# Four layers on one core: where v, the experts' mixing and the first images of layer 3 stand in PE's order

## The chip, the cores and the metric

The kernel runs on one core of a Trainium2 chip. Its engines work side by side and wait for each other through semaphores: PE (TensorE, matrix products), DVE (VectorE), ACT (ScalarE), POOL (GpSimd), and SP (SyncE), which here only issues DMAs. The metric is the time on the device in microseconds, the median of the runs; lower is better.

## The reference

Eight images of 512 channels and 32x32 positions go through four layers, all in f32. Cut to what matters here:

```python
# layer 0: attention with 8 heads, three tanh steps, projection
h = group_norm(x); q, k, v = split(qkv_w @ h + qkv_b)
h = softmax(q k^T * hd**-0.5) v
for _ in range(3): h = h + 0.1 * tanh(h @ inl_w.T + inl_b)
x = x + proj_w @ h + proj_b
# layer 1: one attention over all positions, and x added
x = softmax(q1(x)^T k1(x)) v1(x) + x
# layer 2: up by 2 in both directions (12 taps), leaky relu, down by 2
x = down(leaky_relu(up(x + bias), 0.2) * sqrt(2))
# layer 3: every image has its own weights, mixed from 8 experts
rw = sigmoid(mean(x, positions) @ router_w.T + router_b)     # 8 x 8
W = einsum('be,eoihw->boihw', rw, experts)                   # three convolutions
x = relu(bn3(conv1x1(relu(bn2(conv3x3(relu(bn1(conv1x1(x)))))))) + x)
```

## The kernel before

The program is one straight list for one core. The images are taken in turn through layers 0, 1 and 2. Images 0 to 6 are spilled to DRAM after layer 2; once the last one is through, layer 3 runs over all eight. (A second copy, L53, would run only where an exponential went out of bounds.)

Large products use a scheme of seven half-size products (P1, C11, U2, U3, C22, C21, C12). `product` (L524) does both halves u of each one; `in_turn` (L580) does all seven for u=0, then for u=1, so that its 14 parts can be handed out one by one. It opens one PSUM bank for each of the sums A, X and Y, from `ps_mm`, and yields after each part. U2 and U3 run on X, and U2 is read by DVE before U3 is added to it.

PSUM has three pools of two: `ps_sc` (pairs of banks, 128x1024), `ps_tp` and `ps_mm` (single banks, 128x512). SBUF's large tiles, of 128x4096 words, come from a pool of seven.

Inside `tc.manual_schedule` the order on the named engines is that of the program text. Outside it a planner orders each engine's work by its own costs; layer 0's tanh steps, its projection and layer 1 are such a part.

**Layer 2** (class `Layer2`, L1188) works on quarter tiles of the PE array, 32 or 64 rows by 32 or 64 columns, several of them side by side:

- `wide` (L1196) interpolates along one direction and stores to DRAM (`across`); `turn` (L1219) reads it back with the other direction on the partitions.
- `up` (L1226) interpolates the other direction into two `ps_sc` pairs; ACT multiplies by 0.2 and DVE takes the maximum (L1242, L1243), giving `fine`.
- `down` (L1245) filters and halves `fine` into two `ps_tp` banks; ACT and DVE copy them to `sent` (L1260), and SP stores `sent` in four DMAs to `back`. After four rows `turn_back` (L1267) reads `back` again.
- `narrow` (L1274) filters and halves the other direction into two `ps_tp` banks, which DVE copies (L1290). `channels` (L1292) transposes (`zT`) and sums for the router.

`fine_passes` (L1308) runs eight rows: `up` of row n, a fill, `down` of row n-1, a fill. A fill is one part of other work.

**Images 0 to 6.** `between` (L1324) runs layer 2 of image b and q, k, v of image b+1 in one order. q's parts stand by `wide`. k's 14 parts fill the fine passes, which have 18 fills. Then w_proj is loaded, and v's 14 parts stand around the `narrow` and `channels` passes.

**The last image.** `last_across` (L1375) does `wide` and has the router (L239) compute the gates of images 0 to 6. `last_rows` (L1399) runs the fine passes; their fills are pieces of `blend_early` (L294): 34 products of the gates with 512 columns of the experts' weights (mix, L300), copied by ACT and DVE in turn (L304) and stored by POOL's DMA (L305). `load_experts` reads the experts, 1792 KB at a time, into weight tiles. `last_columns` (L1413) does the narrow passes.

**Layer 3.** `load_weights` (L1479) reads an image's mixed weights, `transform_weights` (L1493) prepares them for the 3x3 convolution by sums of columns. Per image: `c1` (L1522, two halves), `spread` (L1531, four DVE sums of 128x544), four products `c2` (L1541), eight `c3` (L1550). An image's c1 stands in the image before it. The last image's own weights come from `blend_last` (L310), which reads the experts again, two tiles ahead, from products that stand in layer 3's first images.

Of the kernel before, what the change touches and what calls it, by code (L numbers as in the profile page):

```python
# [17 lines left out]
P = 128  # L18
# [39 lines left out]
def tile_sequence(ctx: ExitStack, tc: tile.TileContext, a: dict, out: bass.AP, shifted: bool):  # L58
# [156 lines left out]
    def late_loads():  # L215
# [10 lines left out]
        "early": const.tile([P, EARLY, NR], F32, name="blend_early"),  # L226
        "last": const.tile([P, 2, NR], F32, name="blend_last"),
    }
    nc.gpsimd.memset(blend["last"], 0.0)
    mixed = {  # L230
# [8 lines left out]
    class Router:  # L239
# [28 lines left out]
        def gates(self):  # L268
            at = rw[:, self.images, :]
            nc.scalar.activation(at, at, AF.Sigmoid)  # L270
# [10 lines left out]
    held_experts = []  # L281

    def load_experts():
        i = len(held_experts)
        n = min(len(PARTS) * HALF, WE - i * len(PARTS) * HALF)
        if n <= 0:
            return
        t = wpool.tile([P, len(PARTS), 2, QR], F32, tag="w", name=f"experts_{i}", bufs=3)
        t = t.rearrange("p a b c -> p (a b c)")
        at = i * len(PARTS) * HALF  # L290
        nc.sync.dma_start(t[:, 0:n], a["experts"][:, at : at + n])
        held_experts.append(t)

    def blend_early():  # L294
        rows = EARLY * NR
        op = blend["early"].rearrange("p b g -> p (b g)")
        for i in range(PIECES):
            n, at = divmod(i, len(PARTS))
            ps = bank(name=f"mix_{i}")
            nc.tensor.matmul(  # L300
                ps[0:rows, :], op, held_experts[n][:, ts(at, HALF)], start=True, stop=True
            )
            t = tmp(f"mix_{i}")
            (nc.scalar.copy if i % 2 else nc.vector.tensor_copy)(t[0:rows, :], ps[0:rows, :])  # L304
            nc.gpsimd.dma_start(mixed["early"][:, ts(i, HALF)], t[0:rows, :])  # L305
            if at == len(PARTS) - 1:
                load_experts()
            yield

    def blend_last():  # L310
        per = -(-PIECES // 4)
        op = blend["last"].rearrange("p b g -> p (b g)")
        tiles = {}

        def load(t):
            tiles[t] = big_tile(f"last_experts_{t}", [P, 4, 2 * HALF])
            for c in range(4):
                n = min(2, per - 2 * t, PIECES - per * c - 2 * t)
                if n > 0:
                    at = (per * c + 2 * t) * HALF  # L320
                    nc.sync.dma_start(
                        tiles[t][:, c, 0 : n * HALF], a["experts"][:, at : at + n * HALF]
                    )

        def counts(t):
            return [max(0, min(2, per - 2 * t, PIECES - per * c - 2 * t)) for c in range(4)]

        n_tiles = -(-per // 2)
        for t in range(2):
            load(t)  # L330
        yield
        for t in range(n_tiles):
            counted = counts(t)
            dst = tmp(f"mix_last_{t}", S)
            for i in range(2):
                if not counted[0] > i:
                    continue
                ps = bank(ps_tp, f"mix_last_{t}_{i}")
                last = 0
                for c in range(4):  # L340
                    if counted[c] > i:
                        nc.tensor.matmul(
                            ps[W * c : W * c + W, :], op, tiles[t][:, c, ts(i, HALF)],
                            start=True, stop=True,
                        )
                        last = W * c + W
                nc.scalar.copy(dst[0:last, ts(i, HALF)], ps[0:last, :])
                if i == counted[0] - 1:
                    for c in range(4):
                        n = counted[c] * HALF  # L350
                        at = (per * c + 2 * t) * HALF
                        if n:
                            nc.sync.dma_start(
                                mixed["last"][:, at : at + n], dst[W * c : W * c + NR, 0:n]
                            )
                    if t + 2 < n_tiles:
                        load(t + 2)
                yield
# [221 lines left out]
    def in_turn(name, wt, src, sums_of, made, rows=False, late=False):  # L580

        terms = {
# [8 lines left out]
        for u in range(2):  # L591
            banks = {}
            for what in plain if late and u == 0 else alternate:
# [6 lines left out]
                if what in opens:  # L600
                    banks[opens[what]] = bank(name=f"{name}_{opens[what]}{u}")
# [198 lines left out]
    def layer0(b, q, k, v, w):  # L800
# [193 lines left out]
        next(operators, None)  # L994
        all_of(inner)
        for it in (1, 2):
# [3 lines left out]
            for i, _ in enumerate(parts):  # L1000
                for _ in range(2 if i < 4 else 0):
                    next(operators, None)
        all_of(operators)
        if b + 1 < B:
            w["q"] = weight("q", b + 1)
        else:
            load_experts()
        t = quarter_sums(f"hf_{b}_3", hf)
        all_of(product(f"proj_{b}", w["proj"], hf, t, residual(f"proj_{b}", x)))
        if b + 1 < B:  # L1010
            w["k"] = weight("k", b + 1)
        else:
            load_experts()
        return x

    def layer1(b, x, w, x_next):
# [81 lines left out]
        else:  # L1098
            load_experts()
# [88 lines left out]
    class Layer2:  # L1188
# [85 lines left out]
        def narrow(self, e, i):  # L1274

            banks = [bank(ps_tp, f"narrow_{self.b}_{e}_{i}_{r}") for r in range(2)]
# [12 lines left out]
            for r in range(2):  # L1289
                nc.vector.tensor_copy(t[:, ts(r, HALF)], banks[r])  # L1290
# [17 lines left out]
        def fine_passes(self, fill=lambda: None):  # L1308
            order = [(e, i) for e in range(2) for i in range(4)]
            for n in range(len(order) + 1):  # L1310
                if n < len(order):
                    self.up(*order[n])
                fill()
                if n:
                    e, i = order[n - 1]
                    self.down(e, i)
                    if i == 3:
                        self.turn_back(e)
                fill()
# [4 lines left out]
    def between(b, eT, v, inv, y, x, mv, w):  # L1324
# [3 lines left out]
        with tc.manual_schedule(engines=hand):  # L1328
# [30 lines left out]
            two.fine_passes(lambda: next(parts, None))  # L1359
            all_of(parts)  # L1360
            w["proj"] = weight("proj", b + 1)
            v, parts = values(b + 1, x, t, w)
            steps = [(two.narrow, e, i) for e in (0, 1) for i in range(2)]
            steps[2:2] = [(two.channels, 0, 0), (two.channels, 0, 1)]
            steps += [(two.channels, 1, 0), (two.channels, 1, 1)]
            steps[4:4] = [None] * 3
            for n in range(14):
                if n < len(steps) and steps[n] is not None:
                    steps[n][0](*steps[n][1:])
                next(parts)  # L1370
            all_of(parts)
# [3 lines left out]
    def last_across(b, eT, v, inv, y):  # L1375
        two = Layer2(b)
        act, dve = nc.scalar.copy, nc.vector.tensor_copy
        router = Router(0, EARLY)
        with tc.manual_schedule(engines=hand):
            for what, u in weighted_rows(b, eT, v, inv, y):  # L1380
                if (what, u) == ("P1", 1):
                    router.sums()
                elif (what, u) == ("U2", 0):
                    router.logits()
                elif (what, u) == ("U3", 0):
                    router.gates()
                elif (what, u) == ("U3", 1):
# [4 lines left out]
                elif (what, u) == ("C22", 1):  # L1392
                    router.operator(blend["early"])
            two.wide(1, 1, y, (act, dve))
            two.wide(1, 0, y, (act, dve))
            two.turn(1)
        return two

    def last_rows(two, loads):  # L1399
        with tc.manual_schedule(engines=hand):  # L1400
            mixing, done = blend_early(), 0

            def fill():
                nonlocal done
                for _ in range(2):
                    next(mixing, None)
                done += 1
                loads(done)

            two.fine_passes(fill)  # L1410
            all_of(mixing)

    def last_columns(b, two, aside):  # L1413
        with tc.manual_schedule(engines=hand):
            z = big_tile(f"z_{b}", [P, CC, S])
            aside = aside()
            two.narrow(0, 0)
            two.narrow(0, 1)
            next(aside)
            two.channels(0, 0, z)  # L1420
            two.channels(0, 1, z)
            next(aside)
            two.narrow(1, 0)
            two.narrow(1, 1)
            two.channels(1, 0, z)
            two.channels(1, 1, z)
            all_of(aside)
# [10 lines left out]
    with tc.tile_pool(name=f"weights_{run}", bufs=1) as wpool:  # L1438
# [16 lines left out]
        for b in range(B):  # L1455
# [6 lines left out]
            else:  # L1462
                two = last_across(b, *state)

                def loads(n):
                    if n in (3, 6):
                        i = n // 3 - 1
                        zs[i] = load_z(i)

                last_rows(two, loads)  # L1470

# [50 lines left out]
    def c1(b, g):  # L1522
        ps = bank(ps_tp, name=f"c1_{b}_{g}")
        project(ps, wts[b][:, 0:C].rearrange("p (cc o) -> p cc o", o=P), 0, zs[b], g)
        nc.scalar.activation(
# [73 lines left out]
    mixing = blend_last()  # L1599

    def aside():
        for i in range(2):
            wts[i] = load_weights(i)
        next(mixing)
        yield
        transform_weights(0)
        yield
        for g in range(2):
            c1(0, g)
        spreads[0] = spread(0)  # L1610
        yield

    zs[B - 1] = last_columns(B - 1, two, aside)
    redo = None
    engines = mybir.EngineType
    with tc.manual_schedule(engines={engines.PE, engines.DVE, engines.Activation}):
        router = Router(B - 1, 1)
        router.sums()
        c1(1, 0)
# [3 lines left out]
        for b in range(B):  # L1623
# [10 lines left out]
            next(mixing, None)  # L1634
# [8 lines left out]
            if more:  # L1643
                for g in range(0 if b else 1, 2):
# [8 lines left out]
            if b:  # L1653
                next(mixing, None)
# [76 lines left out]
```

## Time and profile before

| | |
|---|---|
| median of 3 runs | 3623.29 us (3622.79 to 3626.85) |
| profiled execution | 3623.17 us |
| its span, first to last instruction | 3621.4 us |
| PE busy | 3547.8 us (98%) |
| DVE, ACT busy | 2332.5 us (64%), 1316.4 us (36%) |
| mean granted PE clock | 0.996 |
| DMA | 360.86 MB, 100 GB/s in the mean |

A line of the timeline has the start in us, the time until the last of the group ends, the engine, the line of the kernel, the operation, what is written and read, the shape, and how many instructions; in brackets stands how long the engine was idle before it and what ended that. A PE row is half of an f32 product: two rows of 128x512 take 0.86 us. Groups overlap a little, so the time of a group is best taken from start to start. In the waits, a line has who waited for whom, the total in us, how often, and the longest. In the stretches, a line has the length and then, for PE, weight loads, DVE, ACT and POOL, the busy us and (in brackets) the instructions, the granted PE clock, the busy share of the DMA engines, and GB/s.

### The profile page before, as it was taken

The page shows a single profiled execution, that of the slowest core. Times are in us where ns is not written, and L with a number is a line of the kernel's source. Part 1 is how long each engine was busy: PE and PEld are TensorE (multiplying, and loading weights), DVE is VectorE, ACT ScalarE, POOL GpSimd, SP SyncE. Part 2 cuts the span into 40 slices and gives each one's busy share as a digit, 9 for nine tenths or more (in the row PEclk, how much of TensorE's full clock was granted, in tenths as well). Part 3 has the DMA queues.
Part 4 walks back from the last instruction along what each step waited for, and adds up shares of the span by engine and source line. Part 5 has one row for each costly group of instructions (what it writes and reads, how often), then busy time and mean ns, then how long its engine had stood idle before and what let it go on. Part 6 is the DMA issues. An engine that isn't in the chain of part 4 may idle for free.

```text
span 3621.4 us, 47909 instructions
## 1 busy us (share of the span) xinstructions
PE 3547.8 (98%) x19445; PEld 1749.8 (48%) x19445; DVE 2332.5 (64%) x3153; ACT 1316.4 (36%) x1724; POOL 101.6 (3%) x139
## 2 busy tenths in 40 slices
PE   8999999999999999999999999999999999998798
PEld 4346543474435643474535743465434744355343
DVE  4787558765677557765686557774677656765434
ACT  1632345223542246223452236323452235422333
POOL 4000000000000000000000000000000000001100
PEclk9999999999999999999999999999999999999999
DMA  5102441116101341115211350024411261015872
GB/s 202 38 30 85 131 140 42 51 65 196 56 30 71 127 157 42 44 51 166 102 36 64 113 170 21 30 85 134 139 40 64 67 192 45 30 61 193 299 269 108
DMA packets 149032, 360.86 MB, mean 100 GB/s; under 512 B 17792, under 2 KB 92560, under 8 KB 142016
## 3 DMA queue, kind: packets, MB, share of 16 engines
q1 hardware_dynamic: 144336, 338.56, 27.7%
q0 software_dynamic: 4320, 18.87, 1.4%
q8 instruction: 155, 2.54, 0.3%
q14 instruction: 77, 0.63, 0.1%
q10 hardware_dynamic: 144, 0.26, 0.0%
HBM read 226.55 MB, written 118.49 MB: 95 GB/s over the span
## 4 chain that ended last, share of the span: by engine, by line
PE 94%; DMA 2%; DVE 1%; ACT 1%; issue 1%; SPq 0%; POOL 0%; ACTq 0%; POOLq 0%; DVEq 0%
PE scores L830 12%; PE av L875 12%; PE inl_X L555 7%; PE av_X L1177 5%; PE inl_Y L555 4%; PE inl_A L555 4%; PE av_A L1177 3%; PE av_Y L1177 3%; PE v_X L555 3%; PE c L1545 2%; PE proj_X L555 2%; PE v_X L610 2%; PE k_X L610 2%; PE v_Y L555 2%; PE v_A L555 2%; PE q_X L610 2%
## 5 line engine op out<-in xcount | busy, mean ns | idle before, releaser
L849 ACT ACTIVATE e<-scores 128x1024 f32<-128x1024 f32 x504 | 516.6, 1025 | 420.6 <-PE scores L830 368.3
L830 PE MATMUL scores<-q,k 64*64 64x512 f32 x4096 | 530.7, 591 | 0.0
L875 PE MATMUL av<-e,v 64*64 64x512 f32 x4096 | 528.7, 589 | 0.0
L859 DVE TENSOR_TENSOR accs<-accs,e 128x1024 f32<-128x1024 f32 x240 | 294.2, 1226 | 50.8 <-ACT e L849 46.7
L875 PEld LDWEIGHTS av<-e,v 64*64 64x64 f32 x4096 | 156.6, 133 | 282.8 <-issue 274.6
L830 PEld LDWEIGHTS scores<-q,k 64*64 64x64 f32 x4096 | 152.8, 133 | 289.9 <-issue 256.2
L555 PE MATMUL inl_X<-T_hf,w_inl 128*128 128x512 f32 x576 | 262.0, 593 | 0.3 <-DVE inl_U L706 0.3
L1243 DVE TENSOR_TENSOR fine<-up,fine 128x1024 f32<-128x1024 f32 x128 | 150.8, 1220 | 120.5 <-ACT fine L1242 118.2
L695 ACT ACTIVATE inl_U<-inl_U,inl_b 128x512 f32<-128x512 f32 x96 | 66.7, 718 | 305.3 <-DVE inl_U L710 305.3
L555 PEld LDWEIGHTS inl_X<-T_hf,w_inl 128*128 128x128 f32 x576 | 108.6, 190 | 138.9 <-issue 109.7
L555 PE MATMUL inl_A<-hf,w_inl 128*128 128x512 f32 x384 | 174.6, 597 | 0.0
L1242 ACT ACTIVATE fine<-up 128x1024 f32<-128x1024 f32 x128 | 124.1, 1021 | 136.4 <-PE up L1236 121.8
L896 DVE RECIPROCAL inv<-av 128x256 f32<-128x256 f32 x80 | 138.9, 1745 | 0.0
L706 DVE TENSOR_TENSOR inl_U<-inl_X,inl_P 128x512 f32<-128x512 f32 x96 | 61.8, 685 | 106.4 <-PE inl_X L555 106.4
L857 DVE TENSOR_TENSOR accs<-e,e 128x1024 f32<-128x1024 f32 x48 | 59.6, 1242 | 100.2 <-ACT e L849 81.2
L1177 PE MATMUL av_A<-v,eT 128*128 128x256 f32 x512 | 122.6, 383 | 0.0
L555 PEld LDWEIGHTS inl_A<-hf,w_inl 128*128 128x128 f32 x384 | 71.5, 190 | 96.8 <-issue 86.3
L1177 PE MATMUL av_X<-v,eT 128*128 128x256 f32 x512 | 113.9, 381 | 0.0
L1064 ACT ACTIVATE eT<-scores 128x512 f32<-128x512 f32 x128 | 66.1, 602 | 115.4 <-PE scores L382 115.4
L1177 PEld LDWEIGHTS av_X<-v,eT 128*128 128x128 f32 x512 | 96.6, 190 | 19.3 <-DVE av_U L1151 6.5
L1214 ACT COPY wide<-wide 128x1024 f32<-128x1024 f32 x62 | 59.8, 1015 | 122.5 <-PE wide L1206 122.5
L859 DVE TENSOR_TENSOR acc<-acc,e 128x1024 f32<-128x1024 f32 x80 | 96.8, 1210 | 8.4 <-ACT e L849 7.6
(384 smaller groups left out, 5554.6 us busy)
## 6 DMA issues: line engine op xcount, KB each, us to landing
x<-in_x_dram SPq DMA_DIRECT2D x64, 512.0 KB, 6.5
across_u<-wide SPq DMA_DIRECT2D x128, 256.0 KB, 3.7
turned<-across_u SPq DMA_DIRECT2D x64, 512.0 KB, 5.9
back_u<-sent SPq DMA_DIRECT2D x256, 128.0 KB, 2.2
back<-back_u SPq DMA_DIRECT2D x32, 1024.0 KB, 7.7
w_v<-stored_u_v SPq DMA_DIRECT2D x14, 1792.0 KB, 7.3
out_dram<-z SPq DMA_DIRECT2D x31, 512.0 KB, 2.8
spill_u<-z SPq DMA_DIRECT2D x28, 512.0 KB, 5.9
```

What stands on the lines that cost most here:

```text
L555: nc.tensor.matmul(dst, lhs, rhs, start=(opens and s == 0 and cc == 0), stop=(cc == 1 and s == rows), skip_group_check=True,)
L610: nc.tensor.matmul(dst, lhs, rhs, start=(what in opens and s == 0 and cc == 0), stop=(cc == 1 and s == rows), skip_group_check=True,)
L695: nc.scalar.activation(t, ps, AF.Tanh, bias=inl_b[:, c : c + 1])
L830: nc.tensor.matmul(ps[r][rows[c]], k[rows[r], oc, jc * P + c * HD : jc * P + c * HD + HD], q[rows[r], oc, ts(sh, HALF)], start=True, stop= ...
L849: nc.scalar.activation(e, pair, AF.Exp, scale=HD ** -0.5)
L859: nc.vector.tensor_add(accs[g], accs[g], e)
L875: nc.tensor.matmul(avs[g][r][rows[c]], v[rows[r], jc, ts(2 * oc + c, HD)], e[rows[r], ts(c, HALF)], start=(jc == 0), stop=(jc == SC - 1),)
L896: nc.vector.reciprocal(copies[g][:, at], totals[g][:, at])
L1177: nc.tensor.matmul(ps[:, ts(s, QR)], left[:, j, at : at + P], right[:, j, :], start=(what in ("P1", "U2", "C22") and s == 0 and j == 0), s ...
L1242: nc.scalar.mul(t, ps, 0.2)
L1243: nc.vector.tensor_max(t, ps, t)
L1545: nc.tensor.matmul(ps, wts[b][:, at : at + P], spreads[b][:, i, 16 * ky : 16 * ky + HALF], start=(start and ky == 0), stop=(stop and ky == ...
```

## The change

- `fine_passes`: `up`, `down`, then both fills.
- `between`: when k's parts are used up, w_proj is loaded and v's parts go on as fills; after the fine passes the two `narrow` stand together, then two v parts, the two `channels`, two v parts; what is left follows.
- `narrow`: the second of two writes a `ps_sc` pair and is copied by one DVE instruction.
- `in_turn` with `late` (q): its banks come from `ps_mm` and `ps_tp` by turns.
- Router and `blend_early` move from the last rows to layer 0 of the last image: one mixing piece after each part of the second and third tanh steps, three after each part of the projection. The experts go to large tiles of eight pieces, and all copies are ACT's. The operator has all 128 columns.
- The gates are made by exp, an addition and a reciprocal.
- The last rows and columns have as fills parts of layer 3: all of images 0 and 1, and the first c1 half of image 2 (`lean_images`). The z of image 0 and the weights of images 0 and 1 are loaded at the start of `last_across` (z of image 1 at its end), image 2's at the tenth fill, image 3's in the columns. The loop over layer 3 begins with image 2.
- `blend_last` loads one tile ahead and gets three calls per image.

```diff
 def in_turn(...)
+        opened = 0
...
-                    banks[opens[what]] = bank(name=f"{name}_{opens[what]}{u}")
+                    pool = (ps_mm, ps_tp)[opened % 2] if late else ps_mm
+                    opened += 1
+                    banks[opens[what]] = bank(pool, f"{name}_{opens[what]}{u}")
...
 def gates(self):
-            nc.scalar.activation(at, at, AF.Sigmoid)
+            nc.scalar.activation(at, at, AF.Exp, scale=-1.0)
+            nc.vector.tensor_scalar_add(at, at, 1.0)
+            nc.vector.reciprocal(at, at)
...
 def layer0(...)
+        mixing = iter(())
+        if b + 1 == B:
+            router = Router(0, EARLY)
+            router.sums()
+            router.logits()
+            router.gates()
+            router.operator(blend["early"])
+            mixing = blend_early()
+            next(mixing)
         all_of(inner)
         for it in (1, 2):
...
             for i, _ in enumerate(parts):
                 for _ in range(2 if i < 4 else 0):
                     next(operators, None)
+                next(mixing, None)
...
-        all_of(product(f"proj_{b}", w["proj"], hf, t, residual(f"proj_{b}", x)))
+        for _ in product(f"proj_{b}", w["proj"], hf, t, residual(f"proj_{b}", x)):
+            for _ in range(3):
+                next(mixing, None)
+        all_of(mixing)
...
 def blend_early()
-            ps = bank(name=f"mix_{i}")
+            ps = bank(ps_tp, f"mix_{i}")
...
-            (nc.scalar.copy if i % 2 else nc.vector.tensor_copy)(t[0:rows, :], ps[0:rows, :])
+            nc.scalar.copy(t[0:rows, :], ps[0:rows, :])
...
 def narrow(self, e, i)
-            for r in range(2):
-                nc.vector.tensor_copy(t[:, ts(r, HALF)], banks[r])
+            if i == 0:
+                for r in range(2):
+                    nc.vector.tensor_copy(t[:, ts(r, HALF)], banks[r])
+            else:
+                nc.vector.tensor_copy(t, pair)
...
 def fine_passes(...)
                 if n < len(order):
                     self.up(*order[n])
-                fill()
                 if n:
                     e, i = order[n - 1]
                     self.down(e, i)
                     if i == 3:
                         self.turn_back(e)
+                fill()
                 fill()
...
 def between(...)
-            two.fine_passes(lambda: next(parts, None))
-            all_of(parts)
-            w["proj"] = weight("proj", b + 1)
-            v, parts = values(b + 1, x, t, w)
...
+            def fill():
+                nonlocal v, value_parts
+                if next(parts, parts) is parts:
+                    if v is None:
+                        w["proj"] = weight("proj", b + 1)
+                        v, value_parts = values(b + 1, x, t, w)
+                    next(value_parts)
+
+            two.fine_passes(fill)
+            for e in range(2):
+                two.narrow(e, 0)
+                two.narrow(e, 1)
+                for _ in range(2):
+                    next(value_parts)
+                two.channels(e, 0)
+                two.channels(e, 1)
+                for _ in range(2):
+                    next(value_parts)
+            all_of(value_parts)
...
+    def first(b, g):
+        ps = bank(name=f"c1_{b}_{g}")
+        src = wts[b][:, 0:C].rearrange("p (cc o) -> p cc o", o=P)
+        for cc in range(CC):
+            nc.tensor.matmul(
+                ps, src[:, cc], zs[b][:, cc, ts(g, HALF)], start=(cc == 0), stop=(cc == CC - 1)
+            )
+            if cc == 1:
+                yield
+        inner_rim(b, g, ps)
+        if g == 1:
+            spreads[b] = spread(b)
+        yield
+
+    def second(b):
+        main, odd = (bank(name=f"c2_{b}_{i}") for i in range(2))
...
+        c2(b, main, 1, True, False)
+        nc.scalar.copy(one, main)
+        yield
+        c2(b, odd, 3, True, True)
+        yield
+        c2(b, main, 2, False, False)
+        nc.scalar.copy(two, main)
+        nc.vector.scalar_tensor_tensor(one, one, 2.0, two, ALU.mult, ALU.subtract)
+        nc.vector.tensor_add(one, odd, one)
+        nc.scalar.activation(h2[:, ts(1, HALF)], one, AF.Relu, bias=bn[1][1], scale=bn[1][0])
+        yield
+        c2(b, main, 0, False, True)
+        nc.scalar.activation(h2[:, ts(0, HALF)], main, AF.Relu, bias=bn[1][1], scale=bn[1][0])
+        transform_weights(b + 1)
+        yield
+        for oc in range(CC):
...
+            for i in (1, 0):
+                ps = bank(name=f"c3_{b}_{oc}_{i}")
+                nc.tensor.matmul(
+                    ps, wts[b][:, at : at + P], h2[:, ts(i, HALF)], start=True, stop=True
+                )
+                nc.vector.scalar_tensor_tensor(
+                    apart[:, i], ps, scale, apart[:, i], ALU.mult, ALU.add
+                )
+            nc.scalar.activation(dst, dst, AF.Relu, bias=bias)
+            nc.sync.dma_start(out[b, ts(oc, P), :], dst)
+            yield
+
+    LEAN = 2
+
+    def lean_images():
+        transform_weights(0)
+        yield from first(0, 0)
+        for b in range(LEAN):
+            yield from first(b, 1)
+            yield from first(b + 1, 0)
+            yield from second(b)
...
+    last_rows(two, chain, lambda n: load_image(2) if n == 10 else None)
+
+    def more_loads(e):
+        if e == 0:
+            load_image(3)
+            next(mixing)
...
-        for b in range(B):
+        for b in range(LEAN, B):
```

## The prediction

> **What bounds the kernel now.** I read the page's first part and its chain, then PE's waits, then PE's timeline around each wait, and the busy time of stretches of the end. The page:
>
> ```profile
> PE 3547.8 (98%) x19445; PEld 1749.8 (48%) x19445; DVE 2332.5 (64%) x3153; ACT 1316.4 (36%) x1724; POOL 101.6 (3%) x139
> PE 94%; DMA 2%; DVE 1%; ACT 1%; issue 1%; SPq 0%; POOL 0%; ACTq 0%; POOLq 0%; DVEq 0%
> ```
>
> PE sets the end and is idle 73.6 us of 3621.4. Matmul work moved from one place to another gains nothing; only a gap closed does. The waits say where the gaps are (us in total, times, longest):
>
> ```profile
> PE mix L300 <- ACT mix L304: 14.1, 9, 3.6
> PE gn_mean L414 <- DVE mv L396: 10.8, 1, 10.8
> PE dn L1254 <- ACT sent L1260: 10.7, 7, 1.5
> PE narrow L1285 <- DMA back<-back_u: 6.8, 2, 5.8
> PE q_X L610 <- DVE q_U L631: 6.0, 7, 0.9
> PE narrow L1285 <- ACT sent L1260: 5.9, 8, 0.7
> ```
>
> Seven counts are one place in each of images 0 to 6; `mix` and the DMA wait are the last image's. Image 0's place, PE's timeline:
>
> ```profile
> 465.25 1.98 PE L610 MATMUL k_Y<-x,w_k 128*128 128x512 f32 x4
> 467.16 1.11 PE L1236 MATMUL up<-turned,up_v 32*64 32x512 f32 x16
> 468.21 1.09 PE L1254 MATMUL dn<-fine,dn_v 64*32 64x512 f32 x16
> 470.82 2.06 PE L1254 MATMUL dn<-fine,dn_v 64*32 64x512 f32 x16 [1.52 <-ACT sent L1260]
> 473.61 1.19 PE L1285 MATMUL narrow<-back,dn_h 64*32 64x512 f32 x16 [0.73 <-ACT sent L1260]
> 474.74 1.99 PE L610 MATMUL v_A<-w_v,x 128*128 128x256 f32 x8
> 476.66 1.09 PE L1285 MATMUL narrow<-back,dn_h 64*32 64x512 f32 x16
> ```
>
> Between starts a `k` block of four takes 1.91 where four in a run take 1.72: crossing from quarter tiles to full tiles and back costs 0.2. k's 14 parts are used up before the last `dn`, so the two last `dn` and the first `narrow` stand bare: 5.40 from 468.21 to 473.61, for two passes of 1.02. The end, in stretches (busy us by engine, clock, DMA share, GB/s):
>
> ```profile
> 3313.00:3386.00 73.00, 55.48 (x324) 14.77 (x324) 32.14 (x38) 31.16 (x46) 18.72 (x35) 0.93 0.94 335
> 3386.00:3408.00 22.00, 13.53 (x98) 6.46 (x99) 7.41 (x15) 4.23 (x9) 0.23 (x1) 0.77 0.97 337
> 3332.00:3336.00 4.00, 3.47 (x12) 1.14 (x15) 0.69 (x1) 0.97 (x2) 1.44 (x3) 0.57 1.03 419
> ```
>
> In the last image's rows and columns PE idles 17.5 and 8.5, the granted clock drops and the DMA engines are full.
>
> **Images 0 to 6 (seven times).** Before, q's start to the next attention is 107.07 (399.19 to 506.26); fine passes start at 427.12. After: `up` 1.04, `dn` 1.02, two fills together 3.43+0.20=3.63. So up+2 fills 4.67; seven periods of 1.04+1.02+3.63=5.69 are 39.83; dn+2 fills 4.65; sum 49.15. Fills 15 to 18 are v's first four parts. Then per half: two `narrow` 2.04, two v parts 3.56, two `zT` 1.75, two v parts 3.55: 10.90; the second half ends with four v parts (6.92): 14.27. The sum ends at 427.12+49.15+10.90+14.27=501.44, not 506.2: 4.7 each, 33 in all. What could fill it again: (1) `dn` of the last row needs its two maxima, which came 3.6 after `up` (ACT 2x0.97, DVE 2x1.18 behind it); it now starts 4.67 after. (2) `up` needs the score banks back, 3.6 against 4.65. (3) The w_proj load (1792 KB) is now issued ahead of the last row's four back stores on SP, which stand behind it, and the second `narrow` waits for their reload. Before, dn's end to the reload's issue was 4.9 and its landing 5.4 to 8.2 more; PE now arrives 14.5 after dn. That leaves 1.4 to 4.2 for w_proj's effect. Its load began about 5.3 earlier and other weight loads land in 7.3, so stores lose some 2: no stall in the sum; bound 0 to 3 each.
> The wide copy of the second `narrow` (one 1.22 for two 0.69) is on DVE under v parts: 0.
>
> **q's banks.** The wait at q_X is at the fifth row of a block of eight (idle 0.85): U3 accumulates on the bank that DVE is still reading for U2 (0.69). The order U2, U3 stays, and another pool doesn't shorten a read: 0, between -6 (if the wait were for a free bank) and +1.
>
> **Mixing into the last image's inner steps.** 34 pieces of 2x0.429=0.86, 29.2 on PE, go to a stretch that has no gap (3122 to 3210: 88.00 busy of 88): +29.2 there, and off the rows. Loads of 8.9 MB and stores of 7.8 MB move to a DMA share of 0.06. The router goes with it, and there the order costs: PE now has the next step's P1 and the router matmul ahead of inl_X. That P1 reads hf, which DVE writes after its reciprocals and quarter sums: those writes ended at 3126.8, while PE is done at 3122.41. Two router products (0.2 each) come between: P1 starts at 3126.7, idle 4.3, and after the second write and the router matmul (0.3) inl_X is some 4.9 late beyond the work displaced. DVE then makes gates and operator (7x0.17, exp, 14x0.29, some 6) ahead of the U2 sum; PE has X, Y (6.9) to do meanwhile: 0.
> A gap this long also cools the clock. The row: 2.52 of idle before 3332.53 was followed by 3.4 us at half clock (0.57 above), 3.63 and 5.77 by 6.8 and 10.2. [...] By the row 4.3 of idle costs 1.7 to 3.4 (half of 3.4 to 6.8)[...]. I take 2.5. Last, four half-width buffers per piece: copy 0.6, issue 0.53, landing (6.4 when DMA was full, 2.6 at least) give one per 1.1 to 1.9, against one per 1.43 on PE in the proj part: 0 to 9 over 19 pieces, I take 3. Sum: +29.2+4.9+2.5+3=+39.6.
>
> **The last rows and columns.** What fills the gaps is work that stands after 3408 anyway: two images (each 56x0.429=24.0) and two c1 halves. After, from `up` at 3313.09:
> - n=0: 4.67. n=1, n=2: 5.69 each; spread (4x0.72 on DVE) is ahead of the maxima, +1.0.
> - n=3, n=4: fills are three c2 products each, 2.06+5.15+0.2=7.4 each; the last c2 follows a read of its bank (ACT 0.59), +0.8.
> - n=5, n=6: c3 parts. DVE has per period maxima 2.4, four sums of 0.75, half a copy 0.35: 5.7 against PE's 5.69, with two banks between them, and relu (1.15) in front of the next 0.2-multiplication on ACT: 11.4+3.9.
> - n=7: 5.69, n=8: 4.65. Sum 58.3.
> - Columns: two `narrow` 2.04, two c2 products 5.36, two `zT` 1.75, two c2 and two c3 parts with a bank read 9.4, `narrow`'s own bank 0.35: 18.9; then 2.04, two c3 parts 3.65, 1.75: 7.4.
> - c1 of image 2's second half and of 3's first: 6.9.
> So 91.6, where before the first c2 starts at 3417.89, that is 104.8 on. From there before has eight images to go, after six; before: 3621.4-3417.89=203.5. Less two of 24.03+0.3: 154.8. DMA: until image 3's first mixing of last experts some 32 MB must pass, 96 us at 335 GB/s, in SP's order; I have the second experts tile about 6 late at most (one load ahead instead of two): +3. The end: 3313.09+91.6+154.8+3=3562.5, against 3621.4: -58.9. The gates by exp, add, reciprocal: three small operations beside c2, 0.
>
> **Sum.** 3621.4-33.1-58.9+39.6=3569.0. The profiled execution took 3623.17, 1.8 more than its span; its median is 3623.29. So 3571.
>
> **Rivals.**
> - The gaps are worth all they show: no router stall, no cooling, c3 and DMA stalls hidden: 4.9+2.5+3+3.9+3=17 less, 3554. For it: DVE is only 64% busy. Against: [...] both stalls sit on it.
> - DMA bounds the rows: at 94% share it did before, and outputs and weights now come there. 32 MB at 266 GB/s (the mean of 3408 to 3500) take 120 instead of 96; half of the 24 shows: 3583.
> - w_proj holds the back stores in all seven images. It landed in 11.9 (median) before; the stores then land 5 later, the reload is 1.7 to 3 late, seven times: 12 to 21, so 3583 to 3592.
> - Slower: that same load. The margin is about 3.5, the whole gain 52, or 7.5 an image: from a delay of 11 on, the result is slower than before (3623), which needs w_proj's own wait (for PE to be done with k) to be set by a later matmul. Its slot was k's, and k ends two fills earlier; so little chance. 15 would give 3651.
> - The order does nothing: DVE paces the fine passes in images 0 to 6 too. DVE has 2.4+0.35+2x0.7=4.1 per 5.69. Refuted by the rows above, short of a stall I don't see: 3600.
>
> **How the numbers follow.** Mine 0.57, all gaps 0.15, DMA 0.11, w_proj 0.10, passes paced by DVE 0.03, slower 0.03, rest 0.01. Low end: all gaps, 3554, less 1. High end: w_proj's bound, 3592. This leaves out under 0.2. Mine alone: 3561 to 3582. A measurement tells about 0.2% from no change, so faster 0.96, same 0.01, slower 0.03.
>
> **What would show it.** PE busy about 3547 again, idle near 27. The waits dn <- ACT sent and mix <- ACT gone; q_X <- DVE 6.0 as before. Fine periods 5.69 and attention to attention 410.8 for 415.6. A gap of about 4 before the P1 of step 1 in image 7, with half clock after it. DVE named in n=5, n=6 of the last rows. A narrow <- DMA back wait in seven images would prove the rival; a chain with much DMA after 3313 the DMA rival.

## The result, and the profile after

Seven runs of each kernel: 3608.63 us (3602.94 to 3614.95) against 3622.52 us before (3621.00 to 3626.85), a ratio of 0.9963, 95% interval 0.9951 to 0.9974. The change makes the kernel some 14 us faster, where the forecast had some 52 (3571, range 3553 to 3592). The profiled execution took 3608.0 us, with a span of 3606.2.

The page's busy times and its chain, then PE's waits (us in total, times, longest), of the kernel after:

```profile
PE 3537.5 (98%) x19445; PEld 1758.9 (49%) x19445; DVE 2321.4 (64%) x3130; ACT 1318.1 (37%) x1740; POOL 102.1 (3%) x140
...
PE 93%; DMA 4%; DVE 2%; ACT 1%; SPq 0%; issue 0%; DVEq 0%; ACTq 0%
```

```profile
PE narrow L1304 <- DMA back<-back_u: 24.3, 14, 3.3
PE gn_mean L418 <- DVE mv L400: 11.0, 1, 11.0
PE q_X L618 <- DVE q_U L639: 6.0, 7, 0.9
PE c L1656 <- DVE z L1659: 5.2, 3, 2.6
PE inl_A L559 <- DVE hf L700: 3.7, 1, 3.7
```

The waits of `dn` for `sent` (10.7), of `narrow` for `sent` (5.9) and of `mix` (14.1) are gone. In their place stands one wait of 24.3 us for the reload of `back`, fourteen times: twice in each of images 0 to 6. PE still idles 68.7 us, against 73.6 before. The same place in image 0, PE's timeline:

```profile
473.36 1.09 PE L1269 MATMUL dn<-fine,dn_v 64*32 64x512 f32 x16
474.38 1.99 PE L618 MATMUL v_A<-w_v,x 128*128 128x256 f32 x8
...
486.94 1.89 PE L618 MATMUL v_A<-w_v,x 128*128 128x256 f32 x8
489.51 1.09 PE L1304 MATMUL narrow<-back,dn_h 64*32 64x512 f32 x16 [0.69 <-DMA back<-back_u]
493.11 1.96 PE L1304 MATMUL narrow<-back,dn_h 64*32 64x512 f32 x16 [2.50 <-DMA back<-back_u]
495.00 3.78 PE L618 MATMUL v_X<-w_v,T_h 128*128 128x256 f32 x8
```

The last `dn` no longer stands bare: it starts at 473.36 without a wait. But the second half's `narrow` waits twice, and the v part after it takes 3.78 where others take 1.89. That is TensorE at half its clock: the granted clock is 0.50 from 492 to 498. Stretches of 18 us that hold this place in images 0, 2 and 3 (busy us by engine, granted clock, DMA share, GB/s):

```profile
486.00:504.00 18.00, 14.81 (x87) 10.40 (x86) 5.88 (x8) 2.77 (x6) 0.00 (x0) 0.81 0.51 177
...
1325.00:1343.00 18.00, 15.29 (x84) 12.06 (x88) 5.63 (x9) 2.12 (x4) 0.00 (x0) 0.91 0.33 132
1732.00:1750.00 18.00, 15.28 (x109) 11.97 (x109) 7.26 (x10) 3.50 (x7) 0.00 (x0) 1.00 0.54 183
```

Over the seven images these clocks are 0.81, 0.81, 0.91, 1.00, 0.91, 0.91, 0.91. A mean of 0.81 over 18 us is half clock for 6.8 us (images 0 and 1), 0.91 for 3.4 (images 2, 4, 5 and 6). PE is busy for 5.70 and 4.72 us of the two long stretches and throughout the short ones. Half of that busy time, 12.0 us in all, is an estimate of what the clock costs beside the 24.3 of waiting.

Read by stage, from the starts in PE's timeline:

- Images 0 to 6, q's start to the next attention: 107.07 each before; after 108.32, 108.68, 107.86, 105.13, 107.32, 108.07 and 107.24. The sum is 752.6 against 749.5. The forecast had this stage 33.1 shorter; it is 3.1 longer. These 36.2 us are nearly the whole miss: the span is 37.2 over the 3569.0 of the sum.
- From the last image's attention to the end: 621.8 before, 601.8 after; the forecast had 602.5.

### The profile page after: what moved, and what is told of

Read it like the earlier page. It is cut to its first block, busy times and chain, and to the rows that moved or that the text cites. A ratio compares the mean times of both kernels' runs of the same rounds, so it can differ in the third digit from the quotient of the medians.

```text
span 3606.2 us, 47891 instructions
## 1 busy us (share of the span) xinstructions
PE 3537.5 (98%) x19445; PEld 1758.9 (49%) x19445; DVE 2321.4 (64%) x3130; ACT 1318.1 (37%) x1740; POOL 102.1 (3%) x140
## 4 chain that ended last, share of the span: by engine, by line
PE 93%; DMA 4%; DVE 2%; ACT 1%; SPq 0%; issue 0%; DVEq 0%; ACTq 0%
PE scores L838 12%; PE av L883 12%; PE inl_X L559 7%; PE av_X L1192 5%; PE inl_Y L559 5%; PE inl_A L559 4%; PE av_A L1192 3%; PE av_Y L1192 3%; PE v_X L559 3%; PE c L1562 2%; PE proj_X L559 2%; PE k_X L618 2%; PE up L1251 2%; PE v_Y L559 2%; PE dn L1269 2%; PE v_A L559 2%
## 5 line engine op out<-in xcount | busy, mean ns | idle before, releaser
L1192 PEld LDWEIGHTS av_X<-v,eT 128*128 128x128 f32 x512 | 96.6, 190 | 19.3 <-DVE av_U L1166 6.5
```

What stands on the lines that cost most here:

```text
L1192: nc.tensor.matmul(ps[:, ts(s, QR)], left[:, j, at : at + P], right[:, j, :], start=(what in ("P1", "U2", "C22") and s == 0 and j == 0), s ...
```

## The experiments

Each time is a median, with the kernel before timed beside it on the same chip (3622.3 to 3623.8). "Image" is q's start to the next attention in images 0 to 6, and "end" is the last image's attention to the end of the span, both from the profile.

| kernel | us | ratio to before (95%) | image | end |
|---|---|---|---|---|
| before | 3622.9 | | 107.07 | 621.8 |
| after | 3608.6 | 0.9963 (0.9951–0.9974) | 105.1–108.7 | 601.8 |
| late load | 3572.1 | 0.9861 (0.9846–0.9876) | 102.09 | 603.6 |
| load issued by ACT | 3585.6 | 0.9902 (0.9886–0.9917) | 102.3–106.1 | 605.4 |
| before, load early | 3624.1 | 1.0004 (0.9996–1.0013) | 107.07 (two: 107.6, 108.4) | 620.3 |
| tail alone | 3609.7 | 0.9964 (0.9951–0.9978) | 107.07 | 601.9 |
| tail alone, again | 3610.6 | 0.9964 (0.9951–0.9978) | 107.07 | 606.5 |
| before, passes in pairs | 3615.1 | 0.9979 (0.9973–0.9986) | 105.89 | 620.5 |
| late load, passes apart | 3586.8 | 0.9901 (0.9886–0.9916) | 103.6–105.2 | 604.2 |
| late load, q in one pool | 3572.1 | 0.9859 (0.9844–0.9874) | 102.09 | 605.3 |
| images alone | 3613.2 | 0.9973 (0.9962–0.9983) | 105.53 | 622.6 |
| late load, router early | 3570.7 | 0.9857 (0.9842–0.9872) | 102.09 | 602.7 |
| the same, z early | 3564.9 | 0.9838 (0.9824–0.9851) | 102.09 | 596.9 |
| the same, c3 in two pools | 3561.2 | 0.9829 (0.9816–0.9843) | 102.09 | 596.6 |

**The load of w_proj behind the reloads.** My theory after the result: w_proj's 1792 KB, issued on SP just ahead of the last row's four stores, hold those stores and with them the reload. The rival: the new order brings PE to the second half too early whatever the load does.

```diff
                     if v is None:
-                        w["proj"] = weight("proj", b + 1)
                         v, value_parts = values(b + 1, x, t, w)
...
             two.fine_passes(fill)
+            w["proj"] = weight("proj", b + 1)
```

> The kernel after, but w_proj's load stands on SP behind the last row's four back stores and the two reloads of back (where it stood before the change); v's first parts stay in the last rows. Theory A (the load holds the back stores): from dn's end to the reload's issue some 5 us instead of 9.4, PE's wait narrow <- DMA back falls from 24.3 us to under 3, no half clock in images 0 to 6, q's start to the next attention about 102.4 instead of 107.5 in each, 36 us less than after: 3572 to 3576. Rival B (the paired order or the parts of v bring the second narrow too early whatever the load does, or the DMA engines are full anyway): the wait stays above 15 us and the time at 3598 to 3609.

Measured: 3572.1 us, 36.5 under after. The wait for `back` is gone in all images, the clock from 486 to 504 is 1.00, and an image takes 102.09. The chain of the kernel after, in order of time (start us, us, what), shows what the load did:

```profile
476.85 6.90 DMA back_u<-sent
...
484.25 8.72 DMA back<-back_u
...
493.11 1.96 PE narrow L1304 x16
```

A store of 128 KB (median 2.3 us over the whole run) took 6.90, and the reload of `back` could start only then. SP's issues in the two kernels, first after, then with the late load:

```profile
474.43 0.37 SPq L468 DMA_DIRECT2D w_proj<-stored_u_proj  x1
475.33 1.94 SPq L1278 DMA_DIRECT2D back_u<-sent  x4
483.82 1.01 SPq L1287 DMA_DIRECT2D back<-back_u  x2
```

```profile
467.75 9.80 SPq L1278 DMA_DIRECT2D back_u<-sent  x12
479.46 1.00 SPq L1287 DMA_DIRECT2D back<-back_u  x2
480.51 2.03 SPq L468 DMA_DIRECT2D w_proj<-stored_u_proj  x1
```

The last `dn` ended at 474.38 and 474.90, so the reload is issued 9.4 us after it in the one and 4.6 in the other. Over the seven images it is 9.1 to 10.9 against 4.6 to 6.0. The load in question was issued at 474.43, just after `dn` and 0.9 before the stores. Theory A is confirmed and B refuted: PE reaches the second half 14.4 us after `dn` and now waits for nothing.

**The same load in the kernel before.**

```diff
-            two.fine_passes(lambda: next(parts, None))
+            filled = 0
+
+            def fill():
+                nonlocal filled
+                filled += 1
+                if filled == 17:
+                    w["proj"] = weight("proj", b + 1)
+                next(parts, None)
+
+            two.fine_passes(fill)
             all_of(parts)
-            w["proj"] = weight("proj", b + 1)
```

> The kernel before, with nothing changed but w_proj's load, which moves on SP ahead of the last row's back stores (behind the row's before it). Theory A: the load delays the reload there too; before, dn ended at 473, the reload was issued at 477.8 and PE reached the second half at 490.0. Issued some 4.5 us later it lands at 488 to 491, so PE waits 0 to 2 us in each of seven images: 3623 to 3637, and a wait narrow <- DMA back in images 0 to 6. Rival B (the load is no cause by itself): the reload's issue stays at some 5 us after dn, and the time is that of before within 0.1%.

Measured: 3624.1, within the noise of before. The issues on SP are those of after:

```profile
474.23 0.37 SPq L464 DMA_DIRECT2D w_proj<-stored_u_proj  x1
474.70 2.05 SPq L1263 DMA_DIRECT2D back_u<-sent  x4
483.47 1.00 SPq L1272 DMA_DIRECT2D back<-back_u  x2
```

The reload comes 10.1 to 12.2 after `dn`, where it came 4.4 to 5.5 after it before. So the load delays the reload by 5.1 to 7.6 us here, and by 3.6 to 5.7 between the kernel with the late load and after. Before hid nearly all of it, since PE reached the second half 17.1 after `dn`; only the images with 12.2 and 10.9 got longer, by 1.3 and 0.6. After arrives at 14.4 and has both: 2.7 us less slack, and a reload some 4 to 6 us later than before. The time is at the lower end of theory A; B had the same time, but with a reload that stays at 5, which is refuted. By the time alone the two could not be told apart; the reload's issue does it.

**The load on another queue.**

```diff
-                        w["proj"] = weight("proj", b + 1)
+                        w["proj"] = wpool.tile(...)
+                        nc.scalar.dma_start(w["proj"], stored["proj"])
```

> The kernel after, with w_proj's load issued at the same place but by ACT, on another queue than the stores. If it is the order of the queue that holds the stores (they stand behind 1792 KB on the one issuing engine): the reload is issued about 5 to 6 us after dn's end, and the time is 3574 to 3582 (ACT's issue may cost a little). If it is the traffic itself (the 16 DMA engines are busy with the load, whoever issues it): the reload stays some 9 us after dn's end, and the time at 3600 to 3610.

Measured: 3585.6, between the two. The reload is issued 6.6 to 8.5 after `dn`, and PE waits 7.6 for `back` in all, in six places. The comparison is not clean, for two reasons. ACT issued the load at 469.44, five us earlier than SP could, which at that time still stood at the row before's stores. And SP's waits have a line that the edit brought in:

```profile
SPq L1278 <- DMA w_proj<-stored_u_proj: 14.2, 7, 3.1
```

In each of the seven images the third store of the last row was issued only when the load had landed (in image 0 at 478.04 and 478.02), though it reads nothing that the load writes; which of the program's semaphores ties them was not followed up. The first two stores, issued 4.5 to 5.7 us behind the load, took 3.9 to 5.2 us all the same, with the load on ACT's queue. So the issuing queue alone does not explain the late stores; how much falls to the queue, to the traffic and to that wait stays open.

**The last image alone.** Before's order of passes (up, fill, dn, fill: the True below), v's parts and load in images 0 to 6, the rest as after:

```diff
-            v, value_parts = None, None
-            def fill():
...
-            two.fine_passes(fill)
+            two.fine_passes(lambda: next(parts, None), True)
+            all_of(parts)
+            w["proj"] = weight("proj", b + 1)
+            v, parts = values(b + 1, x, t, w)
+            steps = [(two.narrow, e, i) for e in (0, 1) for i in range(2)]
...
```

> The last image's parts alone: the mixing in its inner steps, the router there, the two images' work in its last rows and columns, as after; images 0 to 6 have before's order of passes, of v's parts and of w_proj's load (the banks of q and of narrow as after). My sum gave +39.6 for the mixing and -58.9 for the rows and columns: 19.3 less than before, 3603 to 3604, and q's start to the next attention 107.1 in images 0 to 6. If instead the images' part of the change had brought something and the tail's lost it, this kernel would stand at 3590 or under, or at 3615 or over.

> The same kernel as tail_alone once more, since its profiled execution (3604.2) showed the 19 that my sum had and its four timed ones stood 2 to 7 above it. If the sum's 19.3 holds: median 3603 to 3605. If the last image's part is worth some 13 to 16: 3606 to 3610, and a profile at such a time shows where in the last 600 us the rest goes (a wait for z's load, or half clock after a wait).

Measured: 3609.7 and 3610.6, some 13 us under before, though the first profile (3604.2) shows the end at 601.9, 19.9 shorter. The second profile (3609.8) is at its median and shows where the difference lies. First the one at 3604.2, then the one at 3609.8:

```profile
3364.02 2.31 PE L1615 MATMUL c<-z,weights 128*128 128x512 f32 x4 [0.66 <-DMA z<-spill_u]
3367.63 2.37 PE L1615 MATMUL c<-z,weights 128*128 128x512 f32 x4 [1.30 <-DMA z<-spill_u]
```

```profile
3369.15 5.37 PE L1615 MATMUL c<-z,weights 128*128 128x512 f32 x8 [4.64 <-DMA z<-spill_u]
```

The wait for image 1's z in the last rows is 2.0 in one execution and 4.6 in the other, and with what stands around it this place takes 3.4 more. The rest of the 4.6 between the two ends, 1.2, I put down to the clock; its mean was 0.998 in the first execution and 0.997 in the second. The shares are estimates of mine: half clock in the last rows costs the first 2.9 (the mean from 3300 to 3400 is 0.97), half clock behind the wait of 3.7 at the inner step's P1 costs the second 2.8, so these two cancel, and at a c3 part it costs the second 1.4 more. So the last image's part is worth 20 in one execution, and 13 in the median of this kernel.

**What the images' order is made of.** Passes in pairs alone, in the kernel before:

```diff
                     self.up(*order[n])
-                fill()
                 if n:
...
+                fill()
                 fill()
```

> The kernel before with the passes of images 0 to 6 in pairs (up, dn, then two fills) and nothing else; v's parts stay behind the last rows. By the rows of k (1.91 between two narrow passes, 1.82 and 1.81 in a pair) a period falls from 5.90 to 5.69 in six of the eight periods, since the last two have no fill: 1.2 to 1.3 an image, q's start to the next attention 105.8 for 107.07, and 3613 to 3615 for 3622.9. The waits dn <- ACT sent (10.7) and narrow <- ACT sent (5.9) stay as they are. If pairing is worth nothing alone (the wait of dn for its maxima takes the place of the crossings): 3622 to 3624, and a wait dn <- DVE fine in each image.

Measured: 3615.1, and 105.89 for an image: 1.18 each, as the crossings said. The other way round, the late load with the passes apart again:

```diff
                     self.up(*order[n])
+                if apart:
+                    fill()
                 if n:
...
                 fill()
-                fill()
+                if not apart:
+                    fill()
```

> The kernel after with w_proj's load behind the reloads, as in the run at 3572.1, but the passes of images 0 to 6 apart again (up, fill, dn, fill); v's first four parts stay in the last rows. By the same rows each of seven periods grows by 0.2: 1.4 an image, q's start to the next attention 103.5 for 102.09, 3581 to 3583. v's parts in the gap are then worth 3.5 an image (107.07 to 103.5), 25 in all. If v's parts are worth all of it: 3572.

Measured: 3586.8, 4 over the expected. Images without a wait take 103.6, as expected; four of the seven take 104.3 to 105.2, for a reason that I hadn't worked out: with passes apart a fill more lies ahead of the last `dn`, so PE reaches the second half 12.65 after it, and the reload is late again (narrow <- DMA back 3.9 us, four times). So the 14.4 of the late load leave a margin that a shift of 1.7 uses up in four images of seven.

Then the images' whole order in the kernel before, with the late load but with `narrow`'s and q's banks as before:

```diff
-            two.fine_passes(lambda: next(parts, None))
-            all_of(parts)
+            two.fine_passes(fill, True)
             w["proj"] = weight("proj", b + 1)
...
+            for e in range(2):
+                two.narrow(e, 0)
+                two.narrow(e, 1)
+                for _ in range(2):
+                    next(value_parts)
...
```

> The kernel before with the change's order in images 0 to 6 alone (passes in pairs, v's first four parts in the last rows, the rest two by two) and w_proj's load behind the reloads; q's and narrow's banks, the mixing and the last image as before. My sum had 4.7 an image; the profile of the kernel with the late load showed 4.98 (107.07 to 102.09): 34.9 in seven, 3587 to 3589. Then the last image's part, left over from the run at 3572.1, is worth 15 to 17 in timed runs. If the images' gain leans on the banks or on the moved mixing: 3592 or over.

Measured: 3613.2, where I had 3587 to 3589. An image takes 105.53. The wait of `dn` is gone as in the late load's kernel, and a new one stands at `narrow`, which PE's timeline of image 0 shows:

```profile
476.67 1.09 PE L1285 MATMUL narrow<-back,dn_h 64*32 64x512 f32 x16
478.60 1.68 PE L1285 MATMUL narrow<-back,dn_h 64*32 64x512 f32 x16 [0.84 <-DVE narrow L1290]
480.21 1.99 PE L610 MATMUL v_Y<-w_v,T_h 128*128 128x256 f32 x8
```

Two `narrow` back to back need four banks, and before's pool has two: the second waits for the copies of the first. The pair takes 3.54 and 3.66 here, 1.88 twice with the change's banks. That is 3.44 an image, the whole difference of 105.53 and 102.09. So without the second `narrow`'s tile in the score banks, which I had costed at nothing, 24 of the 35 us are gone, and the order alone brings 1.54 an image. The banks alone bring nothing: the kernel "tail alone" has them with before's order, and takes 107.07. It is the two together that make 4.98.

**q's banks in one pool**, on the kernel with the late load:

```diff
-                    pool = (ps_mm, ps_tp)[opened % 2] if late else ps_mm
+                    pool = ps_mm
```

> The same kernel at 3572.1 with q's banks in one pool as before. My sum: 0, since U3 waits for DVE's read of the very bank that it adds to; the wait q_X <- DVE q_U stays at 6.0 in seven images, 3571 to 3573.5. If the second pool frees something: up to 6 longer, 3578, with a new wait at q_A, q_X or q_Y.

Measured: 3572.1, and q_X <- DVE q_U 6.0 in seven places, as in every kernel here. This part of the change does nothing that a time or a wait shows.

**The last image's two stalls, and a faster kernel.** The router moved into image 7's attention, with the late load:

```diff
+                if b + 1 == B:
+                    routed(i - 20)
...
-            router.sums()
-            router.logits()
-            router.gates()
-            router.operator(blend["early"])
```

> The same kernel at 3572.1 with image 7's router spread over its attention (sums, logits, gates, and one image's operator every second step, from step 20 on) in place of standing at the head of the inner steps. In after, P1 of the first inner step lost 5.45 there: 3.7 of waiting for DVE (hf) and 1.7 at half clock. If the router's work on DVE is what made hf late: the wait inl_A <- DVE hf goes, no half clock follows, 3566 to 3568. If hf is late for another reason (the sum's order, the inner step itself), or the router only moves its stall into the attention, where DVE adds at every step: 3571 to 3575.

Measured: 3570.7, a gain of 1.5 where 4 to 6 were expected. The wait inl_A <- DVE hf is gone, so the router's work on DVE did make hf late. The gain went to the next wait, in the last rows:

```profile
3322.35 1.09 PE L1278 MATMUL dn<-fine,dn_v 64*32 64x512 f32 x16
3328.61 5.95 PE L1629 MATMUL c<-z,weights 128*128 128x512 f32 x8 [5.17 <-DMA z<-spill_u]
```

Part of this 5.2 can be chance: profiles of kernels with the same last rows show this wait at 0.9 to 4.6. The load of z stands on SP behind the reload of the second half. Put ahead of it:

```diff
+            zs[1] = load_z(1)
             two.wide(1, 1, y, (act, dve))
             two.wide(1, 0, y, (act, dve))
             two.turn(1)
-            zs[1] = load_z(1)
```

> The run with the router in the attention (3570.7), where the wait of 3.7 at the inner step's P1 went but one of 5.2 for image 1's z (c <- DMA z<-spill_u, 0.9 in the kernel with the late load alone) came up in the last rows. Here the load of image 1's z stands on SP ahead of the second half's stores of the wide passes in place of behind their reload. If the load's place is what made z late: that wait goes, and the time is 3565 to 3567. If the tail is full of DMA anyway and what is read earlier only pushes the reload of turned back: a wait up <- DMA turned in its place, and 3569 to 3572.

Measured: 3564.9, 5.7 less; the wait for z is gone and none for `turned` came. Last, two pools for the c3 parts of the last rows:

```diff
-                ps = bank(name=f"c3_{b}_{oc}_{i}")
+                ps = bank((ps_mm, ps_tp)[oc % 2], f"c3_{b}_{oc}_{i}")
```

> The same as the run beside it, and the c3 parts of images 0 and 1 in the last rows and columns take their banks from two pools in turn (ps_mm, ps_tp) in place of one. The wait c <- DVE z was 5.2 in three places (the second part waits until DVE has read the first part's two banks); my sum had 3.9 for it. If it is the banks: that wait falls to under 2 and the time by 3 to 5 against the run beside it, 3561 to 3564. If it is DVE's rate (5.7 of DVE for 5.69 of PE in these periods), the wait moves to dn, whose banks the second pool also holds: within 1.5 of the run beside it.

Measured: 3561.2 (3560.0 to 3564.7), against 3562.1 to 3566.7 beside it. The wait c <- DVE z of 5.2 is gone, but the two profiles' ends differ by 0.3 us: the three c3 places are 3.7 shorter, and `dn`, `narrow` and c1 behind them are 3.1 longer. Whether this edit adds anything is not settled. With or without it, this is the fastest kernel of the study, 1.7% under before.

## Why the prediction was wrong

**The step that failed** is the third point of "Images 0 to 6": "Its load began about 5.3 earlier and other weight loads land in 7.3, so stores lose some 2: no stall in the sum". The load didn't begin 5.3 ahead of the stores. SP stood at the row before's stores until 474.3 and issued the load behind them, at 474.43, 0.9 ahead of the last row's first store (0.9 to 1.8 in the seven images). The stores didn't lose 2: the last of the four took 6.7 to 8.2 us, where it took 2.2 before, and the reload came 9.1 to 10.9 after `dn`, for the 4.9 that I had used. With the landing the second half was 3.5 late on average (24.3 in seven images). And the step had no clock in it: the half clock behind these waits cost another 12.0.

Against the 102.09 an image that it takes without the load in front, the stage is 38.0 longer: 24.3 of waiting, 12.0 of half clock, and 1.7 that neither explains (0.3 in image 3, which kept its clock). Against its sum it is 36.2 longer (752.6 for 749.5 less 33.1).

The mechanism stood among the rivals ("w_proj holds the back stores in all seven images"), at 12 to 21 us and one chance in ten. Its own price was too low by the two terms above: 1.7 to 3 an image were taken for waits that measured 3.5, and nothing for the clock. The same prediction priced the clock at image 7's gap, by a row that showed half clock after 2.5 us of idle, and didn't carry that row over to this wait.

**Point by point:**

- 4.7 an image (506.26 less 501.44, its own figures, make 4.8): 4.98 once the load is out of the way. Fine periods 5.69 are as worked out, attention to attention is 410.57 for 410.8. But the sum wrote "two `narrow` 2.04" as if that came with the order; it needs the second pair of banks, and "0" for them was right as a cost and silent on 3.44 of gain.
- q's banks 0: right.
- Mixing in the inner steps, +39.6: the last attention to the first `up` grew by 35.2. The wait of P1 was 3.7 for 4.3, and half clock (3.4 us, PE busy in 2.8 of them) cost 1.4 in that stretch for 2.5; the buffer stalls of 3 hardly showed.
- Rows and columns: 91.6 forecast, 98.9 measured. The clock was at half for some 7 us around the first `up` (mean 0.83 over 20 us), so that n=0 took 7.8 for 4.7. z was 1.0 late. The c3 parts of n=5 and n=6 were about as forecast (15.9 for 15.3), and the columns with the c1 halves behind them took 35.6 for 33.2. The stretch behind took 154.2 for 157.8: the experts' stall of 3 didn't come. These errors and that of the mixing cancel, so that "-19.3" came out at -20.0 in this profile by luck, and it is 13 in the timed runs of tail alone.
- Idle near 27 was forecast; 68.7 measured. The signs named for the rival, "a narrow <- DMA back wait in seven images", are what the profile shows.

On the clock: pairs of waits of 0.69 and 2.50, of 1.99 and 2.11, of 1.06 and 2.10 us (images 0, 1 and 6) were followed by half clock, and one of 0.28 and 2.44 (image 3) was not; the longest single wait of the seven images is 3.34 (image 2). The length of a single wait doesn't price this place; the clocks of the seven stretches do, at an estimated 12.0 us.

## What to carry to other kernels

A large load moved ahead of small stores is priced by what its engine still has to issue in front of it and by what waits behind the stores' landing, not by when the program's text reaches it (here it was issued 0.9 to 1.8 us ahead of the stores, and the last of them took 6.7 to 8.2 us for 2.2); read the issue times of that engine. A wait that appears where there was none can have a second price in the clock; here it was half of the first (12.0 us by the estimate, beside 24.3). And when two pieces of work are put back to back, ask which banks they need before the sum counts them as adjacent: here the order alone brought 1.54 us an image, the banks alone nothing, and both together 4.98.

## What the hardware showed that was not expected

- Half clock followed waits of 2.1 us in image 6 (1.06 some 3 us ahead of it) and not 2.44 in image 3 (0.28 ahead), so the longest wait doesn't sort the images. The two waits together are 3.19, 4.10, 3.82, 2.72, 3.28, 4.03 and 3.16 us in images 0 to 6: least in image 3, which kept its clock. They don't sort how long it lasted: 6.8 us in images 0 and 1, 3.4 in image 2, whose waits are longer than image 0's. No run varied the waits alone, so what decides was not shown.
- The last row's 128 KB stores, issued 0.9 to 3.3 us behind a 1792 KB load, took 6.7 to 8.6 us, about three times the median of 2.3. With the load on another engine's queue the first two still took 3.9 to 5.2.
- The same kernel's end took 601.9 in one execution and 606.5 in another, for one load of z that came later (waits of 4.6 against 2.0) and, by my estimate, for the clock (a mean of 0.997 against 0.998). A profile of one execution can flatter a stage by 5 us.
